# Router logits of four token blocks at once, each in a quarter of the PE array's columns

## The chip, the core and the metric

The kernel runs on one core of a Trainium2 chip. The core has a matrix engine (PE), a vector engine (DVE), a scalar engine (ACT), a general engine (POOL) and a queue engine for transfers (SP). The metric is the time of one execution on the device in microseconds.

## The reference

Four sequences of 2048 tokens with 512 features, all float32. The normalized tokens go to two branches, and the input and both results are added:

```
xn     = layernorm(x)
q,k,v  = xn @ w_qkv                     # 16 heads of 32; q, k also pass a filter over frequencies
out_a  = softmax(q k^T / sqrt(32)) v @ w_out + b_out
logits = xn @ w_gate                    # 8 experts
best   = argmax(softmax(logits)), gate = its probability
place  = running count of tokens of that expert; kept if below 100
out_f  = gate * (token @ w_expert + b_expert) for kept tokens, else 0
result = x + out_a + out_f
```

The change concerns the line with `logits`: for each sequence a product of 2048 x 512 by 512 x 8.

## The kernel before, in words

The program is one long unrolled list. Normalized tokens of one sequence stand transposed in `xnT`: 128 features in the partitions, four groups of features (`NR`), 2048 tokens. The 16 heads are taken in four groups of four heads, so there are 16 head groups (four for each sequence), and each of them goes through its queries in four blocks of 512. One block is worked off in eight **windows** of two key tiles each: 16 x 4 x 8 = 512 windows, some 9 us each, and 32 windows to a head group. Windows of a group are counted here from 0.

In a window, for each of the two key tiles, PE computes scores of two heads at a time (`shift`, `scores`) and, beside them, other scores whose maxima are needed ten windows later (`max_matmuls`); ACT exponentiates the scores into the tiles `even` and `odd`; DVE takes the maxima (`max_reduce`, tile `part`); PE multiplies by the values (`products`), which DVE adds to `num`. POOL issues the transfer that adds `odd` into `even` (`pair`, 1 MB) and adds `even` tiles to each other (`add_to`), except in the third window of each block.

Everything else is on an **agenda**: a list of small steps for each window. One half of a window's steps is issued after its first key tile and the other half after its second. On PE, DVE, ACT and POOL instructions keep this order exactly (`InOrder`). Transfers issued by SP are placed by the planner of the framework. The steps that matter here:

- `projections`: twelve steps for each head group, a query, key or value block each. `columns` writes four heads of 32 columns into four quarters of the output partitions, so four matmuls use four column groups of the array. Each step has 16 matmuls of 512 columns (or 64 of 128).
- `turn`: transposition of the normalized tokens into `xnT`.
- the steps of `close_steps` after each block: `fold` sums the weights on PE; `fetch`, `invert`, `spread` bring the row sums through memory to their reciprocal (the tiles `sums`, `few`, `inverse`, `factor`); `divide` forms `ot`, `result` projects it on PE, `add` sends it off.
- `max_close`: maxima of a block to the row `negm` of the coming windows.
- the **route** of a sequence: `score`, five steps; then `below_top`, `divide`, `best`, `ranked`, `first_best`, `place`, `carry_on`, `locate`, `note`; then 16 `enter`, one indirect transfer each, which write the tokens' numbers and gates into the tables of the experts. The steps stand in successive windows. For the first sequence they begin in window 8 of head group 0 (`at(NW + i, step)`), for the others in window 10 of the last head group of the sequence before (`at(start + 10 + i, follow_route, i)`); `xnT` is complete by then.

`score(n)` computes block n's logits with experts in the partitions and tokens along the row, four accumulating matmuls whose stationary side is `w_gate` (128 x 8); ACT copies the result to `byx`. The next step transposes it in four pieces of 8 x 128 to have tokens in the partitions, and DVE copies the piece to `logits`. `below_top` then subtracts the largest logit: DVE finds it, POOL subtracts, ACT exponentiates.

PSUM has eight banks of 512 columns. `bank()` hands them out in turn (`turns`), and nothing else decides which bank a step gets. `joined` takes the maximum of two neighbouring banks in one DVE instruction, and of banks 7 and 0 in two.

Of the kernel before, what the change touches and what calls it, by code (L numbers as in the profile page):

```python
# [12 lines left out]
F32 = mybir.dt.float32  # L13
# [9 lines left out]
H, DH = 16, 32  # L23
NF = DH // 2 + 1
E, CAP = 8, 100
P = 128
NT = S // P
NR = DM // P
HG = P // DH
NG = H // HG  # L30
QB = 512
NQ = S // QB
TQ = QB // P
# [68 lines left out]
def attention_and_top1_experts(ctx: ExitStack, tc: tile.TileContext, a: dict, out: bass.AP):  # L102
    nc = tc.nc
# [4 lines left out]
    const = ctx.enter_context(tc.tile_pool(name="const", bufs=1))  # L108
# [8 lines left out]
    def bank():  # L117

        return array[:, next(turns), :]
# [12 lines left out]
    ident, upto, same_head = (square[:, j, :] for j in range(3))  # L132
# [24 lines left out]
    work = ctx.enter_context(tc.tile_pool(name="work", bufs=2))  # L157
# [33 lines left out]
    on = SimpleNamespace(tensor=nc.tensor, vector=nc.vector, scalar=nc.scalar, gpsimd=nc.gpsimd)  # L191
# [20 lines left out]
    def token_stage(b):  # L212
# [4 lines left out]
        held = {}  # L217
# [37 lines left out]

        logits = small.tile([P, NT, E], F32, name="logits")

        def score(n):
            if n > 0:
                pg = bank()  # L260
                for t in range(TQ):
                    on.tensor.transpose(
                        pg[:, t * E : (t + 1) * E], held["byx"][0:E, t * P : (t + 1) * P], ident[0:E, 0:E]
                    )
                on.vector.tensor_copy(
                    logits[:, (n - 1) * TQ : n * TQ, :], pg[:, 0 : TQ * E].rearrange("p (t e) -> p t e", e=E)
                )
            if n < NQ:
                pg = bank()
                for r in range(NR):  # L270
                    on.tensor.matmul(
                        pg[0:E, :],
                        lhsT=w_gate[:, r, :],
                        rhs=xnT[:, r, n * QB : (n + 1) * QB],
                        start=(r == 0),
                        stop=(r == NR - 1),
                    )
                held["byx"] = work.tile([P, QB], F32, tag="byx", name="byx", bufs=1)
                on.scalar.copy(held["byx"][0:E, :], pg[0:E, :])

        full = [P, NT, E]
        probs = small.tile(full, F32, name="probs")
# [78 lines left out]
        def enter(i):  # L361
            on.gpsimd.indirect_dma_start(
                tables[i % NTAB],
                bass.IndirectOffsetOnAxis(ap=slot[:, i : i + 1], axis=0),
                entry[:, i, :],
                None,
                bounds_check=SLOTS - 1,
                oob_is_err=False,
            )

        route = [lambda n=n: score(n) for n in range(NQ + 1)]
        route += [below_top, divide, best, ranked, first_best, place, carry_on, locate, note]
        route += [lambda i=i: enter(i) for i in range(NT)]
        return load, measure, scale, normalize, turn, route, bias, first_sums

# [4 lines left out]
    def load_qkv_weights(k):  # L380
        wg[k] = weights.tile([P, NR, 3, P], F32, name="wg", bufs=1)
        nc.sync.dma_start(out=wg[k], in_=wd[k % NG])
# [303 lines left out]


    load, measure, scale, normalize, turn, first_route, first_bias, first_sums = token_stage(0)
    for n in range(NQ):
        tiles = range(n * TQ, (n + 1) * TQ)  # L690
# [8 lines left out]
        if n == 0:  # L699
            filter_weights(0)  # L700
            load_qkv_weights(0)
    w_gate = const.tile([P, NR, E], F32, name="w_gate")
    nc.scalar.dma_start(out=w_gate, in_=a["L0_ffn_w_gate"].rearrange("(r p) e -> p r e", p=P))
    b_out = const.tile([P, DM], F32, name="b_out")
    nc.scalar.dma_start(out=b_out, in_=a["L0_attn_b_out"].partition_broadcast(P))

# [45 lines left out]
    def begin_stage(b):  # L752
        stage["all"] = token_stage(b)
# [176 lines left out]
```

## Time and profile before

| | us |
|---|---|
| median of three runs (lowest, highest) | 4603.65 (4592.69, 4610.5) |
| the profiled execution | 4607.95 |
| its span, first to last instruction | 4606.1 |
| PE busy | 4435.0 |
| DVE busy | 3102.1 |
| POOL busy | 3001.0 |
| ACT busy | 2596.2 |
| mean granted PE clock | 0.984 |

In a line of a group or of the timeline, `array<-xnT,w_gate 128*8 128x512 f32` is a matmul that writes PSUM (`array`) from the moving side `xnT` and the stationary side `w_gate`: 128 rows and 8 columns of the array are used, and 512 columns of moving data stream through it. A float32 matmul leaves two records, a transposition one or two. Groups give busy time (overlaps counted once), mean duration of one in nanoseconds, and idle time before them. Since matmuls overlap, busy time divided by the number of records is what one of them occupies. Most instructions carry line 82, that of the helper `InOrder`, so the names of the tiles tell what a line is. `square` is the tile with the identity in it, so a matmul from `square` is a transposition.

### The profile page before, as it was taken

How to read it: one execution, taken by the hardware profiler on the slowest of the kernel's cores; microseconds unless marked ns; L12 is line 12 of the kernel's file. 1: busy time of each engine (PE TensorE's matmuls, PEld its weight loads, DVE VectorE, ACT ScalarE, POOL GpSimd, SP SyncE). 2: the span in 40 equal slices, each digit the busy share in tenths (PEclk: the TensorE clock that was granted, in tenths of full speed). 3: DMA queues.
4: the chain of work that ended last, by engine and by line, in shares of the span. 5: the costliest groups of instructions: out<-in, count | busy, mean ns of one | idle time of the engine just before them, and what ended most of it. 6: DMA issues, size and time to landing. Idle time of an engine off the chain costs nothing.

```text
span 4606.1 us, 106228 instructions
## 1 busy us (share of the span) xinstructions
PE 4435.0 (96%) x44438; PEld 1886.8 (41%) x44438; DVE 3102.1 (67%) x3625; ACT 2596.2 (56%) x4945; POOL 3001.0 (65%) x2081
## 2 busy tenths in 40 slices
PE   6999999989999999998999999999999999999986
PEld 3444443433434344443444434343343434434431
DVE  4666776765676767775567766776567676777772
ACT  3445555555555555556455555555555565555654
POOL 0467766765676666775577666767567675777766
PEclk9999999989999999999999999999999999999998
DMA  5567777886776877787577776878767776787876
GB/s 117 137 153 149 152 157 149 186 184 137 142 151 140 163 147 159 151 205 177 120 145 154 158 154 134 165 163 191 158 125 150 155 152 127 151 169 163 162 159 143
DMA packets 193234, 708.90 MB, mean 154 GB/s; under 512 B 47778, under 2 KB 54084, under 8 KB 127344
## 3 DMA queue, kind: packets, MB, share of 16 engines
q0 software_dynamic: 110576, 606.88, 66.6%
q1 hardware_dynamic: 77800, 91.56, 6.4%
q8 instruction: 348, 5.70, 0.5%
q10 hardware_dynamic: 4376, 3.67, 0.4%
q14 instruction: 134, 1.10, 0.1%
HBM read 77.09 MB, written 89.99 MB: 36 GB/s over the span
## 4 chain that ended last, share of the span: by engine, by line
PE 85%; DMA 7%; POOL 3%; issue 3%; ACT 1%; DVE 1%; SPq 0%; ACTq 0%; POOLq 0%; DVEq 0%
PE array L82 85%; DMA even<-odd 2%; POOL even L82 2%; DMA few<-sums 1%; DMA sums<-den 1%; DMA negm<-row 1%; DVE part L82 1%; ACT odd L82 1%; DMA wg<-wd 0%; POOL ot L82 0%; DMA wd<-in_L_attn_w_qkv_dram 0%; POOL table L82 0%; ACT even L82 0%; PE array L393 0%; POOL rest L82 0%
## 5 line engine op out<-in xcount | busy, mean ns | idle before, releaser
L82 DVE TENSOR_REDUCE part<-array 128x2 f32<-128x1024 f32 (+1 forms) x2312 | 2433.6, 1097 | 1271.2 <-PE array L82 1259.4
L82 POOL TENSOR_TENSOR even<-even 128x1024 f32<-128x1024 f32 x892 | 2179.2, 2568 | 218.9 <-DMA even<-odd 217.0
L82 PE MATMUL array<-k,q 32*128 32x512 f32 x8192 | 2233.1, 623 | 8.5 <-issue 4.7
L82 PE MATMUL array<-q,k 32*128 32x512 f32 x8192 | 2059.8, 596 | 1.4 <-issue 1.4
L82 ACT ACTIVATE even<-array 128x512 f32<-128x512 f32 x2048 | 1065.4, 601 | 506.0 <-PE array L82 484.6
L82 ACT ACTIVATE odd<-array 128x512 f32<-128x512 f32 x2048 | 1060.7, 602 | 451.7 <-issue 237.7
L82 POOL DMA_DIRECT2D even<-odd x511 | 463.9, 908 | 1149.1 <-ACT odd L82 929.7
L82 PEld LDWEIGHTS array<-k,q 32*128 32x128 f32 x8192 | 812.1, 184 | 196.8 <-issue 76.1
L82 PE MATMUL array<-negm,ones_b 3*128 3x512 bf16 x4096 | 800.9, 383 | 55.7 <-DMA negm<-row 29.4
L82 PEld LDWEIGHTS array<-q,k 32*128 32x128 f32 x8192 | 752.1, 186 | 13.9 <-issue 5.1
L82 DVE TENSOR_TENSOR num<-num,array 128x512 f32<-128x512 f32 x960 | 651.1, 678 | 63.0 <-PE array L82 46.5
L82 PEld LDWEIGHTS <-ones_b 3*128 3x128 bf16 x4096 | 204.0, 92 | 926.8 <-issue 781.6
L82 PE MATMUL array<-even,v 128*32 128x512 f32 x4096 | 549.5, 609 | 9.8 <-ACT odd L82 9.7
L82 PE MATMUL array<-odd,v 128*32 128x512 f32 x4096 | 550.4, 608 | 3.3 <-ACT even L82 3.1
L82 PE MATMUL array<-xnT,wg 128*32 128x512 f32 x4032 | 461.6, 592 | 2.2 <-DMA wg<-wd 1.2
L82 PE MATMUL array<-wo,ot 128*32 128x512 f32 x2048 | 258.7, 596 | 19.6 <-POOL ot L82 19.5
L82 PEld LDWEIGHTS array<-xnT,wg 128*32 128x32 f32 x4032 | 131.8, 110 | 304.5 <-issue 268.8
L82 PEld LDWEIGHTS array<-even,v 128*32 128x32 f32 x4096 | 80.9, 108 | 400.8 <-ACT odd L82 388.2
L82 PEld LDWEIGHTS array<-odd,v 128*32 128x32 f32 x4096 | 81.3, 108 | 399.2 <-ACT even L82 388.5
L82 PEld LDWEIGHTS array<-wg,xnT 128*32 128x32 f32 x8192 | 226.1, 110 | 38.1 <-issue 22.6
L82 ACT COPY y<-array 128x512 f32<-128x512 f32 x252 | 147.5, 586 | 163.4 <-PE array L82 163.2
L82 PE MATMUL array<-wg,xnT 128*32 128x128 f32 x8192 | 237.0, 273 | 0.5
(140 smaller groups left out, 1436.0 us busy)
## 6 DMA issues: line engine op xcount, KB each, us to landing
even<-odd POOLq DMA_DIRECT2D x511, 1024.0 KB
out_dram<-y POOLq DMA_DIRECT2D x63, 1024.0 KB
xs<-in_L_attn_x_dram SPq DMA_DIRECT2D x31, 1024.0 KB
out_dram<-xs SPq DMA_DIRECT2D x16, 1024.0 KB
factor<-inverse SPq DMA_DIRECT2D x252, 64.0 KB
wg<-wd SPq DMA_DIRECT2D x16, 768.0 KB
wo<-in_L_attn_w_out_dram SPq DMA_DIRECT2D x16, 256.0 KB
negm<-row SPq DMA_DIRECT2D x192, 4.0 KB
```

The source lines that it names most:

```text
L82: done = act(*args, **kwargs)
```

## The change

`w_gate` is widened from 8 to 32 columns, of which 24 are zero; it is filled with zeros by POOL before the transfer. `score` becomes one step that goes through all four blocks: for each group of features it issues four matmuls, block n writing partitions 32n to 32n + 31 of one bank, so that each block uses its own quarter of the array's columns. ACT copies the whole bank to `byx`, in which block n's logits of the eight experts are in partitions 32n to 32n + 7. A second step, `by_token`, makes four transpositions of 128 x 128 and copies the useful columns to `logits` in one DVE instruction. The route is three steps shorter, and all that follows the logits stands three windows earlier.

```diff
-        def score(n):
-            if n > 0:
-                pg = bank()
-                for t in range(TQ):
-                    on.tensor.transpose(
-                        pg[:, t * E : (t + 1) * E], held["byx"][0:E, t * P : (t + 1) * P], ident[0:E, 0:E]
-                    )
-                on.vector.tensor_copy(
-                    logits[:, (n - 1) * TQ : n * TQ, :], pg[:, 0 : TQ * E].rearrange("p (t e) -> p t e", e=E)
-                )
-            if n < NQ:
-                pg = bank()
-                for r in range(NR):
+        def score():
+
+            pg = bank()
+            for r in range(NR):
+                for n in range(NQ):
                     on.tensor.matmul(
-                        pg[0:E, :],
+                        pg[DH * n : DH * (n + 1), :],
                         lhsT=w_gate[:, r, :],
                         rhs=xnT[:, r, n * QB : (n + 1) * QB],
                         start=(r == 0),
                         stop=(r == NR - 1),
                     )
-                held["byx"] = work.tile([P, QB], F32, tag="byx", name="byx", bufs=1)
-                on.scalar.copy(held["byx"][0:E, :], pg[0:E, :])
+            held["byx"] = work.tile([P, QB], F32, tag="byx", name="byx", bufs=1)
+            on.scalar.copy(held["byx"], pg)
+
+        def by_token():
+            pg = bank()
+            for t in range(TQ):
+                at = slice(t * P, (t + 1) * P)
+                on.tensor.transpose(pg[:, at], held["byx"][:, at], ident)
+            on.vector.tensor_copy(
+                logits.rearrange("p (n t) e -> p n t e", t=TQ),
+                pg.rearrange("p (t n e) -> p n t e", t=TQ, n=NQ)[:, :, :, 0:E],
+            )
...
-        route = [lambda n=n: score(n) for n in range(NQ + 1)]
-        route += [below_top, divide, best, ranked, first_best, place, carry_on, locate, note]
+        route = [score, by_token, below_top, divide, best, ranked, first_best, place, carry_on, locate, note]
         route += [lambda i=i: enter(i) for i in range(NT)]
...
-    w_gate = const.tile([P, NR, E], F32, name="w_gate")
-    nc.scalar.dma_start(out=w_gate, in_=a["L0_ffn_w_gate"].rearrange("(r p) e -> p r e", p=P))
+
+    w_gate = const.tile([P, NR, DH], F32, name="w_gate")
+    nc.gpsimd.memset(w_gate, 0.0)
+    nc.scalar.dma_start(out=w_gate[:, :, 0:E], in_=a["L0_ffn_w_gate"].rearrange("(r p) e -> p r e", p=P))
```

## Prediction, made before the changed kernel ran

> **What bounds the kernel now.** I read the page's busy shares and chain first, then the table of stretches around the router's five windows, then the groups of instructions by shape, then the timeline of one window, and last the waits of ScalarE.
>
> From the page: the busy line, and the chain that ended last.
>
> ```profile
> PE 4435.0 (96%) x44438; PEld 1886.8 (41%) x44438; DVE 3102.1 (67%) x3625; ACT 2596.2 (56%) x4945; POOL 3001.0 (65%) x2081
> ...
> PE 85%; DMA 7%; POOL 3%; issue 3%; ACT 1%; DVE 1%; SPq 0%; ACTq 0%; POOLq 0%; DVEq 0%
> ```
>
> PE carries 85% of the chain. An average could still hide a stage where another engine decides, so here are the second sequence's five router windows (the third and fourth look alike):
>
> ```profile
> 1063.40:1077.40 14.00, 14.00 (x108) 4.77 (x107) 5.97 (x8) 6.04 (x12) 5.48 (x5) 1.00 0.95 203
> 1077.40:1091.00 13.60, 13.60 (x108) 4.83 (x106) 5.04 (x6) 5.69 (x11) 1.92 (x1) 1.00 0.52 103
> 1091.00:1101.10 10.10, 10.10 (x72) 3.51 (x68) 5.93 (x8) 4.65 (x10) 5.55 (x3) 1.00 0.51 105
> 1101.10:1114.70 13.60, 13.60 (x104) 4.60 (x100) 6.31 (x9) 5.31 (x11) 5.57 (x3) 1.00 0.46 99
> 1114.70:1121.70 7.00, 7.00 (x69) 3.23 (x65) 6.52 (x9) 4.45 (x9) 5.57 (x3) 1.00 0.72 150
> ```
>
> Columns: stretch, length, then busy time of PE, weight loads, DVE, ACT, POOL, then PE's clock and the DMA share. PE is busy in every microsecond at full clock; the next engine has 6.52 of 7.00 in the shortest window and over 4 us of slack in the long ones. Time taken off PE here comes off the clock until a window nears 6.5 us. The groups by shape say what PE spends on the router:
>
> ```profile
> L82 PE MATMUL array<-xnT,wg 128*32 128x512 f32 x4032 | 461.6, 592 | 2.2 <-DMA wg<-wd 1.2 <-DVE part L82 1.0
> L82 PE MATMUL array<-xnT,w_gate 128*8 128x512 f32 x128 | 57.6, 592 | 0.0
> L82 PE MATMUL array<-square,xs 128*128 128x128 f32 x192 | 28.3, 290 | 19.0 <-DVE part L82 19.0
> L82 PE MATMUL array<-square,byx 8*128 8x8 f32 x64 | 6.6, 207 | 0.0
> ```
>
> The router's 64 matmuls leave 128 records (two each) and take 57.6 us: 0.45 each. The projections (first row) have the same 592 ns per record and occupy 461.6/4032 = 0.114 each: four run side by side, in four column groups. The timeline gives start to start:
>
> ```profile
> 1065.55 1.06 PE L82 MATMUL array<-odd,v 128*32 128x512 f32 x8
> 1066.43 3.60 PE L82 MATMUL array<-xnT,w_gate 128*8 128x512 f32 x8
> 1069.96 0.39 PE L82 MATMUL array<-negm,ones_b 3*128 3x512 bf16 x2
> ...
> 1072.99 3.62 PE L82 MATMUL array<-xnT,wg 128*32 128x512 f32 x32
> 1076.42 1.04 PE L82 MATMUL array<-even,ones 128*32 128x512 f32 x8
> ```
>
> Eight router records hold PE for 1069.96 - 1066.43 = 3.53 us; 32 records in four column groups for 1076.42 - 1072.99 = 3.43. The eight "odd,v" records take 0.88 us, that is 0.11 each too, and there, as in the change, each column group streams its own moving data.
>
> **What the Trainium skill says.** "TensorEngine Tiling (Array Packing)", section Performance Considerations, gives 4x column tiling for a stationary side of 32 columns or fewer. The trace agrees: 32 records cost what eight did. "TensorE: Matmul & The Clock Gate", Part 3, is more careful (2.38x measured for three column tiles); for streams of 32 the projections' rows show nearly the full four, and I use those. The tiling page's Key Properties say that a change of tiling mode drains the array. The trace shows about 0.1 us: products to the next matmul take 0.88 us before others of their own kind and 1.00 before row-tiled ones. Part 1 of the TensorE page says that ScalarE's queue is strict FIFO; the stall below shows it.
>
> **The change, part by part, for one sequence.**
> 1. Removed: four bursts of eight records, 4 x 3.53 = 14.1 us; four sets of four 8-row transpositions, 0.34 us each (the timeline has 0.34 from the first of a set to the burst behind it), 1.4 us. Sum 15.5.
> 2. Added: 16 matmuls are 32 records at 0.107 = 3.43 us. Four 128 x 128 transpositions: 28.3/192 = 0.147 each, 0.6 us with a drain. Sum 4.05. Saved 11.4 us; four sequences 45.8 us. Weight loads grow from 8 to 32 columns (89 to 110 ns) and lie beside the matmuls, as the projections' do.
> 3. ACT: one copy of 128 x 512 (0.585) for four of 8 x 512 (0.575), 1.7 us less. DVE: one 128 x 128 copy from PSUM (nearest row 0.29, a tensor operation of that size) for four of 0.184, 0.4 us less. Both at nothing: PE is longer in these windows. `by_token` waits for the copy, which is issued a window earlier.
> 4. Start: a memset of 128 x 128 on POOL (the same shape, `ones`, took 0.20 us) ahead of the w_gate transfer. POOL is idle from 1.3 to 26.4 us, the transfer is issued at 33.7 and first needed at 205.8. Nothing. On SP and POOL the change adds and removes no transfer.
> 5. PSUM turns: two banks are taken instead of eight, so later tiles sit two banks further. A pair of maxima is split in two where it wraps from bank 7 to 0: now 264 of 2048 (528 halves), cost 2 x 0.683 - 1.220 = 0.15 us of DVE each. A tile takes nine banks, so the parity alternates and the share stays at about one in eight. Nothing; even 60 more are 9 us of DVE beside PE.
> 6. Moved: all that follows the logits comes three windows earlier, with each of its instructions, the 16 indirect transfers too. On POOL these pass one window's additions more or less; the same sums stay, but one wait changes. `below_top` has ACT wait for POOL's subtraction, which is queued behind POOL's two additions (5 us). The waits have it (total, times, longest), and the timeline of ACT, then of PE, in the second sequence:
>
> ```profile
> ACT probs L82 <- POOL probs L82: 18.5, 4, 5.4
> ```
>
> ```profile
> 1123.00 2.06 ACT L82 ACTIVATE even<-array 128x512 f32<-128x512 f32 x4 [0.97 <-PE array L82]
> 1130.51 0.31 ACT L82 ACTIVATE probs<-probs 128x128 f32<-128x128 f32 x1 [5.45 <-POOL probs L82]
> 1130.73 0.57 ACT L82 COPY k<-array 128x512 f32<-128x512 f32 x1
> ```
>
> ```profile
> 1131.35 0.69 PE L82 MATMUL array<-k,q 32*128 32x512 f32 x1 [0.96 <-ACT k L82]
> ```
>
> Behind the waiting activation stand the copy of k and the exponentials, and PE at last finds no free bank. It costs PE 2.10 us in sequence 1 and 0.96, 0.47 and 0.46 in the others, 4.0 in all; the last three had a projection in the same half window to go on with. After the change sequence 1 does it in window 10, where POOL does no additions (0.22 us busy now): 0. The others do it in the thirteenth window of their group, a bare one with additions, as sequence 1 has it now: 2.10 each, 6.3. So +2.3; bounds -4 and +8 (each of four at 3 us).
> 7. Its rows for `best`, `first_best` and `place` meet other neighbours. A window of 6.3 us with 0.6 us more on DVE can go over by some tenths. Zero taken; bounds -1 (the last entry, now in a window that idles PE for 1.35 us, may free it) and +6.
>
> Sum: -45.8 + 2.3 = -43.5. The profiled execution took 4607.95 us (span 4606.1 and 1.85 around it), 4.3 above the median of three, 4603.65, whose runs spread over 18 us; so 4564.5 by its own time and **4560 us** against the median.
>
> **Rivals.**
> - *Half is eaten* (0.10). Shorter windows uncover POOL and DVE: five windows lose 11.4 of 58.3 us and keep their 29.8 us of DVE and 24.1 of POOL. Against: the sum, 46.9, stays far above both. It would need about 5 us of new stall a sequence: 4583.
> - *No overlap* (0.04). The four column groups run one after another, since each streams other tokens. 16 x 0.9 us stays, the transpositions save 0.8, four times: 4601. Against: the "odd,v" row.
> - *Slower* (0.05): SP's transfers are ordered by the planner, not pinned like the four compute engines, and the planner sees other durations. If it puts the read-back of the row sums (few<-sums) behind a load of 1 MB, DVE waits at its reciprocal; maxima and PE wait behind it. That happens now: 67.0 us of DVE's waits, 13 times, the longest 13.7, with 6.4 us of PE idle in a window. At 6.5 us for PE each, the 43.5 are gone after 7 more of the 63 closings, and 4627 (over 0.5% slower) is reached at 10 more. For: such order has no fixed place. Against: no transfer changes, and after the five windows each step keeps its neighbours on the planned agenda.
>
> The main case has 0.81, by itself 4548 to 4574. **Range 4546 to 4582**: its upper end takes in the bounds of 6 and 7 and most of the first rival, its lower end the lower bounds and the spread of the runs. 0.5% is 23 us, about what a measurement of this kernel tells from no change. Faster by more: the main case and half of the first rival, 0.86. Within: the rest of it and the second, 0.09. Slower: 0.05.
>
> **What would show it.** PE's busy time falls by about 46 us to 4390. A w_gate group of 128 records of the form 128*32 occupies about 14 us, not 57.6; the group with byx has 16 records and about 2.4 us. The second sequence's five windows take about 47 us. ACT still waits for POOL's probs, about 3 us each time. Wrong, if the w_gate records start 0.43 us apart one by one; if PE's idle time (171 us now) grows by over 15; or if the waits for few<-sums go well beyond 67 us.

## The result and the profile after

| | before | changed |
|---|---|---|
| median of four runs each, us | 4601.88 (4592.69 to 4610.5) | 4547.28 (4539.47 to 4548.28) |
| profiled execution, its span | 4607.95, 4606.1 | 4547.31, 4545.5 |

The ratio is 0.9875, with a 95% interval of 0.9854 to 0.9896: the changed kernel is faster by 48 to 67 us, 57 by the ratio and 54.6 by the medians. The forecast was 43.5. The direction holds, and so do the steps that were priced, each within some 2 us; the gain is larger than their sum by 11 to 14 us, and that part is what most of the experiments are about.

The page of the changed kernel, busy times and the chain that ended last:

```profile
PE 4381.8 (96%) x44390; PEld 1877.2 (41%) x44390; DVE 3099.6 (68%) x3609; ACT 2590.4 (57%) x4933; POOL 3002.4 (66%) x2082
...
PE 85%; DMA 7%; POOL 3%; issue 2%; ACT 2%; DVE 1%; ACTq 0%; POOLq 0%; SPq 0%; DVEq 0%
```

PE is still the bound. Its busy time fell by 53.2 us, 7 more than was forecast, and its idle time from 171.1 to 163.7. The groups by shape:

```profile
L82 PE MATMUL array<-xnT,w_gate 128*32 128x512 f32 x128 | 14.5, 592 | 0.0
L82 PE MATMUL array<-square,byx 128*128 128x128 f32 x16 | 2.6, 286 | 0.0
```

The router's 128 records occupy 14.5 us instead of 57.6, the transpositions 2.6 instead of 6.6. In the timeline the 32 records of the second sequence are followed by the next matmul after 1050.73 - 1047.18 = 3.55 us:

```profile
1047.18 3.62 PE L82 MATMUL array<-xnT,w_gate 128*32 128x512 f32 x32
1050.73 0.39 PE L82 MATMUL array<-negm,ones_b 3*128 3x512 bf16 x2
```

The five windows of that sequence, by stretches with the columns as before:

```profile
1044.20:1058.20 14.00, 14.00 (x133) 5.12 (x134) 5.96 (x7) 6.00 (x12) 5.45 (x5) 1.00 0.97 207
1058.20:1068.60 10.40, 10.40 (x99) 4.08 (x95) 5.09 (x6) 5.05 (x10) 1.89 (x1) 1.00 0.65 131
1068.60:1077.20 8.60, 6.37 (x64) 2.36 (x62) 6.53 (x9) 4.20 (x10) 5.91 (x4) 1.00 0.60 122
1077.20:1086.90 9.70, 9.70 (x96) 3.73 (x93) 6.20 (x9) 4.86 (x10) 5.97 (x4) 1.00 0.67 137
1086.90:1094.40 7.50, 7.50 (x65) 3.12 (x61) 7.13 (x11) 4.75 (x10) 5.56 (x3) 1.00 0.70 142
```

They take 50.2 us instead of 58.3. The third one is the only one in which PE is idle, by 8.60 - 6.37 = 2.23 us. It is the stall at `below_top`, in its new window, of the size that the forecast gave it. ACT's and PE's timelines have it in the form that was seen before:

```profile
1069.87 2.08 ACT L82 ACTIVATE even<-array 128x512 f32<-128x512 f32 x4 [1.02 <-PE array L82]
1075.33 0.31 ACT L82 ACTIVATE probs<-probs 128x128 f32<-128x128 f32 x1 [3.38 <-POOL probs L82]
```

```profile
1076.17 1.06 PE L82 MATMUL array<-even,v 128*32 128x512 f32 x8 [2.23 <-ACT odd L82]
```

**Where the rest came from.** I set the two traces side by side window by window, each of the 512 from the first `shift` matmul to that of the next. The thirteen windows of each route from the logits on give 13.9, 10.1, 9.3 and 8.2 us less, 41.5 together; the forecast was 43.5. Another 17 us are lost before the change in seven windows in which it does nothing: 50, 146, 148, 211, 306, 308 and 336 of the 512. They are shorter by 1.6, 1.7, 3.8, 2.0, 5.0, 1.9 and 0.9, 16.8 together. The other windows' differences nearly cancel (waits for the rows `negm` and row sums move by up to 6 us each way). Window 306 of the kernel before, on PE:

```profile
2812.23 0.38 PE L82 MATMUL array<-negm,ones_b 3*128 3x512 bf16 x1
2815.56 0.37 PE L82 MATMUL array<-negm,ones_b 3*128 3x512 bf16 x1 [2.96 <-issue]
...
2816.73 1.94 PE L82 MATMUL array<-even,v 128*32 128x512 f32 x8
2818.43 1.87 PE L82 MATMUL array<-even,ones 128*32 128x512 f32 x8
```

The same window in the changed kernel:

```profile
2767.91 0.38 PE L82 MATMUL array<-negm,ones_b 3*128 3x512 bf16 x2
...
2769.09 1.07 PE L82 MATMUL array<-even,v 128*32 128x512 f32 x8
2769.97 1.04 PE L82 MATMUL array<-even,ones 128*32 128x512 f32 x8
```

Before, PE stood still for 2.96 us between two matmuls of one pair, "issue" being all that the profile can name; and the two groups behind it came at half their pace, 1.94 and 1.87 us for what takes 1.07 and 1.04. The profile names no data and no bank that it waited for. The pages' lines for the queue that brings PE's instructions are, before and changed:

```profile
q8 instruction: 348, 5.70, 0.5%
```

```profile
q8 instruction: 347, 5.69, 0.5%
```

5.70 MB for the 88,876 records of PE and its weight loads are 64 bytes each, and a packet, 5.70 MB / 348 or 16.4 KB, holds 256 of them: **blocks of 256 instructions**. In the trace's packet records a block arrives from 2813.1 to 2814.1, and PE goes on 1.5 us later. In each of the seven windows a block arrives in this way, 1.3 to 1.5 us ahead of the end of the wait. And if all of PE's records (matmuls, weight loads and semaphore instructions) are counted from the first on, the last record ahead of the pause is number 193 of 256 in every one of the seven. All seven pauses lie in or behind a value step of `projections` (128 records with 128 weight loads, in 3.7 us). PE uses 19 instructions in a microsecond on average and 70 in such a step, so that it goes through a whole block there in less than 4 us. And the change takes out 24 instructions per sequence, so that all later ones stand 24, 48, 72 or 96 places earlier in the blocks. That is theory A: the instructions taken out moved the value steps off places at which PE runs dry. Rivals: the PSUM banks (B), since later tiles sit two banks on, and chance of transfers (C).

### The profile page after: what moved, and what is told of

Its sections match the earlier page's. It is cut to its first block, busy times and chain, and to the rows that moved or that the text cites. A ratio compares the mean times of both kernels' runs of the same rounds, so it can differ in the third digit from the quotient of the medians.

```text
span 4545.5 us, 106083 instructions
## 1 busy us (share of the span) xinstructions
PE 4381.8 (96%) x44390; PEld 1877.2 (41%) x44390; DVE 3099.6 (68%) x3609; ACT 2590.4 (57%) x4933; POOL 3002.4 (66%) x2082
## 4 chain that ended last, share of the span: by engine, by line
PE 85%; DMA 7%; POOL 3%; issue 2%; ACT 2%; DVE 1%; ACTq 0%; POOLq 0%; SPq 0%; DVEq 0%
PE array L82 85%; DMA even<-odd 3%; POOL even L82 2%; DMA few<-sums 1%; DMA negm<-row 1%; ACT odd L82 1%; DMA sums<-den 1%; DVE part L82 1%; DMA wg<-wd 0%; POOL ot L82 0%; DMA wd<-in_L_attn_w_qkv_dram 0%; ACT even L82 0%; PE array L394 0%; POOL table L82 0%; ACT xs L82 0%
## 5 line engine op out<-in xcount | busy, mean ns | idle before, releaser
L82 PE MATMUL array<-even,v 128*32 128x512 f32 x4096 | 547.2, 606 | 15.5 <-ACT odd L82 15.4
```

The lines of the kernel that those rows point to most:

```text
L82: done = act(*args, **kwargs)
```

## Experiments

All times are medians; ratios are to the kernel before, run beside each.

| kernel | us | before, us | ratio (95%) |
|---|---|---|---|
| changed | 4547.28 | 4601.88 | 0.9875 (0.9854 to 0.9896) |
| before_pad226 | 4591.17 | 4606.31 | 0.9966 (0.9953 to 0.9979) |
| before_turn2 | 4605.35 | 4606.31 | 0.9998 (0.9987 to 1.0009) |
| after_pad48 | 4579.78 | 4606.31 | 0.9941 (0.9926 to 0.9955) |
| after_pad256 | 4549.14 | 4606.31 | 0.9875 (0.9861 to 0.9890) |
| after_same_places | 4569.68 | 4604.32 | 0.9917 (0.9901 to 0.9932) |
| after_serial | 4570.06 | 4603.42 | 0.9920 (0.9892 to 0.9949) |
| after_one_group | 4596.54 | 4604.32 | 0.9981 (0.9970 to 0.9992) |
| after_in_place | 4542.57 | 4603.42 | 0.9860 (0.9826 to 0.9895) |
| after_split | 4544.58 | 4603.42 | 0.9864 (0.9833 to 0.9894) |

**Shifting PE's instructions, with nothing else.** The edit, with N = 113, 24 and 128; no other instruction and no order on any engine changes. PE waits for its first data at that time, and the 113 took 3.2 us of that wait.

```diff
+    for _ in range(N):
+        nc.tensor.matmul(array[0:DH, 7, 0:DH], lhsT=ones_b[:, 0:DH], rhs=ones_b[:, 0:DH], start=True, stop=True)
     eps = const.tile([P, 1], F32, name="eps")
```

before_pad226:

> The kernel before, with 113 small bf16 matmuls (226 PE instructions) put ahead of everything else on PE, where it waits for its first data until 8.8 us. No other instruction and no order changes; only the place of each PE instruction in the blocks of 256 in which PE's instructions are fetched is shifted. Theory A (the gain beyond the forecast is instruction fetch: value steps that begin at place 157 to 187 of a block run PE dry in windows 15 to 20 of a head group): none of these steps stays at such a place with long stalls, so about 10 us faster than before, and the issue waits of 1 to 3 us in windows 146, 148, 211, 306, 308 and 336 are gone. Rival B (the PSUM turns did it): no change. Rival C (chance of transfers): no change beyond 4 us.

after_pad48:

> The changed kernel with 24 small bf16 matmuls (48 PE instructions) ahead of everything on PE. Theory A: the value steps in windows 146, 148, 210, 212, 402 and 434 move to places 155 to 188 of a block, and PE runs dry there for 1 to 3 us each: 8 to 14 us slower than the changed kernel, its gain on before falls to about 43 us. Rivals B and C: the same time as the changed kernel within 4 us.

after_pad256:

> Control: the changed kernel with 128 small matmuls (256 PE instructions, one whole block) ahead of everything on PE. The places in the blocks are those of the changed kernel again. Theory A: the time of the changed kernel within 3 us (about 55 us below before). If more instructions as such cost time, 5 us or more slower than the changed kernel.

226 idle instructions make the kernel before faster by 0.34%, some 16 us, where 10 were expected, and 48 of them make the changed kernel slower by some 30 us, where 8 to 14 were expected; 256, one whole block, leave it where it was. So it is the place in the block that counts here and not the number of instructions, and rival C, which foresaw no change in the first two, falls. Windows 50, 146, 148, 211, 306, 308 and 336 of before_pad226 are 14.9 us shorter than those of the kernel before. The pauses are not all gone, as the expectation had it: one of 1.7 us is left in window 146 (put down to ACT by the profile, but behind the same record 193), and windows 82, 246, 377, 404 and 436 are longer by 1.4 to 1.7 each. In after_pad48 windows 146, 148, 402, 404, 434 and 436 are longer than in the changed kernel by 3.3, 3.6, 5.7, 3.8, 4.6 and 1.9. The expectation had named 210 and 212 too and left out 246 (3.5 us longer), 404 and 436; one stall came a window behind (211). In all eleven traces, with the idle instructions counted in, 71 pauses of more than 0.7 us between two starts stand behind the same record 193 of 256: 9 in the kernel before, 3 in the changed one, 11 in after_pad48, 4 in after_pad256. In each of the 71, PE goes on 1.2 to 1.6 us after a block has landed. PE's waits for "issue" (total, times, longest), for before, before_pad226, changed and after_pad48:

```profile
PE array L82 <- issue: 10.3, 8, 3.0
```

```profile
PE array L82 <- issue: 6.4, 10, 1.3
```

```profile
PE array L82 <- issue: 1.3, 4, 0.4
```

```profile
PE array L82 <- issue: 14.6, 13, 2.1
```

They rise and fall with the times, but hold only a part of it: the matmuls behind a pause can also come at a slower pace, as in window 306, and count as busy then. In the seven windows PE is busy for 7.1 us less in the changed kernel than before, about the 7 us by which its busy time fell more than was forecast. Why the pace is slower was not tried.

**The banks.** Two more turns behind each sequence's last score step, so that later tiles sit where they sit in the changed kernel:

```diff
             if n > 0:
...
+                if n == NQ:
+                    next(turns), next(turns)
```

> The kernel before, with the PSUM turns moved two banks on after each sequence's last score step, so that later tiles sit in the banks that they have in the changed kernel; no instruction is added on PE. Theory A: same as before within 3 us. Rival B (the new banks are what brought the part of the gain that was not forecast): about 11 us faster than before.

No change, 0.9998. Rival B falls.

**The change with the old places.** 24 instructions per sequence are put back as idle ones:

```diff
         def by_token():
             pg = bank()
+            for _ in range(12):
+                on.tensor.matmul(pg[0:DH, 0:DH], lhsT=ones_b[:, 0:DH], rhs=ones_b[:, 0:DH], start=True, stop=True)
```

> The changed kernel with 12 small bf16 matmuls (24 PE instructions, 27 ns a pair where they stood at the start of PE, so some 0.3 us) at the head of each by_token. The change had taken out 24 PE instructions per sequence; now each later PE instruction stands at the place in its block that it has in the kernel before, to one or two. Theory A (fetch): the waits for instructions in windows 50, 146, 148, 211, 306, 308 and 336 come back, 12 to 17 us, and with 1.3 us for the matmuls themselves the time is 4560 to 4566, that is 40 to 45 us below before: the forecast without its error. Rival C (chance of transfers): 4549, 1.3 us above the changed kernel, and none of these windows differs.

The ratio rises from 0.9875 to 0.9917: 0.42%, 19 us, come back (7 to 31 with both intervals), of which the 48 small matmuls themselves should be 1.3. The seven windows are longer again by 1.4, 3.4, 1.9, 1.9, 4.5, 1.3 and 1.0, 15.5 together. By the ratio the kernel is 38 us faster than before (31 to 46), where the forecast's sum with these matmuls is 43.5 - 1.3 = 42.2. The median, 4569.68, is 4 us above what was expected. The value steps stand at the kernel before's places to one or two, and window 306 looks as it did there:

```profile
2781.15 0.70 PE L82 MATMUL array<-k,q 32*128 32x512 f32 x2 [2.70 <-issue]
...
2782.22 1.78 PE L82 MATMUL array<-even,v 128*32 128x512 f32 x8
2783.76 1.96 PE L82 MATMUL array<-even,ones 128*32 128x512 f32 x8
```

**The columns.** First the loops exchanged, at the same number and places of instructions:

```diff
-            for r in range(NR):
-                for n in range(NQ):
+            for n in range(NQ):
+                for r in range(NR):
```

> The changed kernel with the two loops of score exchanged: block outside, features inside, so that the 16 matmuls come four at a time on one column group and can't run side by side. Same instructions, same number, same places in the fetched blocks. Theory (the columns side by side are the gain that was forecast): 32 records at 0.43 us instead of 0.107, 10.3 us more in window 8 or 10 of each sequence's route, 41 us in all, near 4588. Rival (the gain lies in the transpositions, the shorter route or the fetch): within 10 us of the changed kernel.

It missed: the window with the logits is longer by 5.2 us in each sequence, not 10.3, and the time by some 21 by the ratios. So this order did not put the matmuls one after another, and the four blocks were given one column group in a second run:

```diff
-            pg = bank()
-            for r in range(NR):
-                for n in range(NQ):
+            for n in range(NQ):
+                pg = bank()
+                for r in range(NR):
                     on.tensor.matmul(
-                        pg[DH * n : DH * (n + 1), :],
+                        pg[0:DH, :],
...
-            on.scalar.copy(held["byx"], pg)
+                on.scalar.copy(held["byx"][DH * n : DH * (n + 1), :], pg[0:DH, :])
+            for _ in range(5):
+                next(turns)
```

> The changed kernel with all four blocks in the first column group, one after another, in four banks and with four copies to byx; number and places of PE instructions stay. The exchanged loops of after_serial left half of the matmuls side by side (5.2 us more per sequence, not 10.3), because a block's first four records ran beside the last four of the block before. On one column group nothing can run beside: theory 10.3 us more in window 8 or 10 of each route, 41 us in all, near 4588. If the array had another way to overlap them, 5 us as in after_serial, 4570.

Each of the four windows is longer by 11.0 us, 44 in all, and the median by 49; the other 5 us lie in other windows and are not explained. The groups, first after_serial, then after_one_group:

```profile
L82 PE MATMUL array<-xnT,w_gate 128*32 128x512 f32 x128 | 35.3, 595 | 0.0
```

```profile
L82 PE MATMUL array<-xnT,w_gate 128*32 128x512 f32 x128 | 55.6, 592 | 0.0
```

One column group occupies 55.6 us, as the kernel before did with 57.6; four side by side 14.5. This 41 us is the gain that the forecast was built on.

**Moving and splitting `below_top`.**

```diff
-        route = [score, by_token, below_top, divide, ...
+        route = [score, by_token, *[lambda: None] * 3, below_top, divide, ...
```

> The changed kernel with three empty steps ahead of below_top, so that below_top and all behind it stand in the windows that they had before the change. The forecast's step 6: PE loses 2.10, 0.96, 0.47 and 0.46 us at below_top again instead of 0.37, 2.23, 2.17 and 2.22, so some 2 to 3 us faster than the changed kernel, which a time can't tell but the windows can. Rival (the earlier route is a part of the extra gain): 5 us or more slower.

The time can't tell it from the changed kernel. The windows can: the 2.2 us of three sequences are gone, and the windows where `below_top` stood before are longer again by 2.0, 1.5 and 1.5 us (their PE idle time shows 0.9 and twice 0.4 of it). In sequence 1 PE is idle for 4.80 us in window 13, where the kernel before had 2.10. So the earlier route costs or brings next to nothing, and it is no part of the extra gain.

```diff
             on.gpsimd.tensor_tensor(probs, logits, wide(top), ALU.subtract)
+
+        def exponentiate():
             on.scalar.activation(probs, probs, AF.Exp)
...
-        route = [score, by_token, below_top, divide, ...
+        route = [score, by_token, below_top, exponentiate, divide, ...
```

> The changed kernel with below_top cut in two: maximum and subtraction as before, the exponential on ACT one window later, when POOL has long done the subtraction. If ACT's wait for POOL's probs is what idles PE in the window of below_top, the idle 2.2 us of three sequences go and the kernel is 5 to 7 us faster than the changed one (4541). If the stall only moves on (bank or DVE), the same time.

The stall is gone. The third stretch of the second sequence, 8.60 us in the changed kernel with 6.37 of PE, is now:

```profile
1075.90:1082.20 6.30, 6.30 (x61) 2.35 (x59) 6.11 (x9) 4.16 (x9) 5.49 (x4) 1.00 0.72 146
```

These windows of the three sequences are 2.3 us shorter each, and two more behind them 0.5 to 0.8 each. The median is 2.7 us lower, within the interval. In the profiled execution part of it was lost again: with `place` one window later, window 15 of the first sequence waits 3.6 us for the rows `negm`. Whether this version is faster than the changed one stays open.

## Why the prediction was right or wrong

- **The bound.** Right: PE ended the chain, and time taken off it in the route's windows came off the clock.
- **Steps 1 and 2.** Right: 14.5 us for the matmuls (14 forecast) and 2.6 for the transpositions (2.4). after_one_group shows that this is the columns' doing. In after_in_place, where nothing behind the logits has moved, the five windows of each sequence are shorter by 44.2 us in all, for 45.8 forecast.
- **Steps 3 and 4.** As far as ACT, DVE and the memset go, right: nothing of theirs shows. Step 4's sentence that the change adds and removes no transfer was said of SP and POOL, and this is the step that failed: it put what the removed instructions change in PE's own stream at nothing, without a reason. PE has a queue of its own for its instructions, and 24 instructions fewer per sequence shift every later one in its blocks. That term was missing from the sum. It measured 19 us by ratios (the changed kernel against after_same_places; 18 without the small matmuls), 17 in the seven windows of the profile. With it the sum is 43.5 + 17, 60.5 us; the profiled executions differ by 60.6. That these agree to a tenth is luck: the routes' windows gave 41.5 instead of 43.5, and what the other windows lost and won happens to leave 2. After_same_places, without it, is where the forecast's own terms lead, within its interval.
- **Step 5.** Right: before_turn2 moved the banks and nothing happened.
- **Step 6.** Right in the place and size of the new stalls, wrong in the price: 2.23, 2.17 and 2.22 us for 2.10 each, 0.37 for 0 in sequence 1. The stalls of before were larger than their idle time (after_in_place has 2.0 for 0.96), so the price was about zero, not 2.3.
- **Step 7.** Right: `best` makes its window 7.2 to 7.5 us long, where after_in_place, without it there, has 6.7 to 7.0 (DVE has 7.13 in the second sequence's), and `place` moves its 4.0 us from one window to another.
- **The rivals.** Half eaten: no; the five windows of the second sequence took 50.2 us for the 46.9 of the forecast, and 2.23 of the 3.3 between are a stall that was foreseen. No overlap: no. SP's order: the same transfers in the same order, but for three small reads of the tables some 3500 us after the start; few<-sums cost DVE 63.6 us instead of 67.0.
- **The range.** Its lower end, 4546, was put there for small bounds and the spread of runs. The result, 4547, sits at that end, below the 4548 of the main case, for a reason that the range did not know; that it lies inside the range is luck.

## What to carry to other kernels

Column groups side by side made four matmuls cost what one had, with each group streaming its own data; a PE-bound kernel gives back what is taken from PE, provided that the neighbours in those windows are read too. Taking PE instructions out or putting them in also shifts all later ones in the blocks in which they are fetched, and here that was worth 16 us one way (226 idle ones) and some 30 the other (48), more than half of what the change itself brought. So before a change of one per cent in a long unrolled program is explained, it is run once more with idle instructions ahead of it: a whole block as the control, a part of one as the test.

## What the runs showed of the hardware that was not expected

- PE ran dry for 1.2 to 3.3 us, from one start to the next, in the seven windows of the kernel before. In six of them a value step began at places 152 to 180 of 256 (the expectations count seven places further), in window 50 at place 120; such a step uses up a block in 3.7 us. Not every step at such a place ran dry: in window 248 of the kernel before, at place 164, the next block began to arrive 0.6 us after the step's first matmul and nothing was lost, while in the seven it began to arrive 3.1 to 5.9 us after it. What delays the fetch there, whether it is asked for late or waits behind the 1 MB transfers that are at work in these windows, was not tried.
- In after_serial PE started matmuls of one token block beside those of the token block before. The starts of the first records are 0, 0.43, 0.86, 1.29, 1.72, 1.72, 2.15 and 2.18 us: from the fifth on in pairs. The eight records of a token block use one column group, and in after_one_group all 32 records of one column group follow each other at 0.43 us. So the first record of a later token block started before the last three of the one in front of it; this is worked out from the starts, since the records don't name their column group. The Trainium skill ("TensorE: Matmul & The Clock Gate", Part 1, Architectural detail) describes PE's queue as a partial reorder window that pulls weight loads ahead of matmuls in flight; here the matmuls' starts, too, depart from the order of the program. How far ahead PE looks was not tried.
- A small bf16 matmul of 32 columns with its weight load took 28 ns in a row of 113 (3.2 us).
